# 3x3 taps on TensorE as 64x32 and 32x32 tiles over pairs of rows, one ring of seven PSUM banks, and selections moved in front of the 3x3 evictions

## The chip, the cores and the metric

The kernel runs on one core of a Trainium2 chip. The metric is the device time of one execution in microseconds (us). The kernel before was run three times: 7173.82, 7131.42 and 7154.4 us, median 7154.4. One further execution was profiled, and all traces and rows come from it.

## What is computed

The input x has 8 images of 32 channels and 128x128 pixels. All arithmetic is float32.

```
y  = group_norm(x)                    # 16 groups of 2 channels
xb = for each pixel, the K=8 shifted copies of y (5x5 window) whose 3x3 patches
     differ least: channels 32*8 = 256
h  = relu(dw3x3(conv1x1(xb, w1), w2)) # 256 -> 256 channels, then 3x3 per channel
h  = relu(dw3x3(conv1x1(h, w3), w4))
wi = sigmoid(dw3x3(conv1x1(h, w5), w6))
x1 = x + conv1x1(grouped1x1(wi * grouped1x1(xb, dct_w), inv_dct_w), agg_w)
out = x1 + conv5x5(group_norm(x1), kernel)   # the same 5x5 kernel for all channels
```

## The kernel before, in words

**Steps and turns.** An image is cut into 16 stripes of 8 rows (R), and a 17th, short step (n = NS = 16) finishes the rows that the 3x3 convolutions still owe. That makes 136 steps, 128 of them full. The main loop (L918 on) runs over the steps s, and in each step over four turns, i in (3, 2, 1, 0). Turns 3, 2 and 1 are the three conv layers, each on another stripe: layer 1 on step s, layer 2 on step s-1, layer 3 on step s-2. Turn 0 ends stripe s-2: the dct product (`final_dct`, L747), then, in the next turn, the aggregation and the addition (`final_add`, L763).

**A conv layer.** The 1x1 convolution has 256 output channels. Channels 128 to 255 ("v") are made by `pointwise_v` (matmuls L637 into banks `pv`, ACT's copies L645 into the buffer `tv`), and their 3x3 taps run on DVE: the first tap is an ACT activation (L685), the other eight are DVE instructions (L688), and an activation on ACT (L692) ends them. Channels 0 to 127 ("t") are made by `pointwise_t` (matmuls L660 into banks `p`, ACT's copies L667 into the buffer `t`), and their 3x3 taps run on TensorE (`depthwise_t`, L700 on): the partitions of `t` hold four rows of 32 channels each, and the weights `dwd` are diagonal blocks over 96 or 128 partitions, so that a matmul with 32 output columns sums three vertical taps at once. Each bank `pw` holds four of the stripe's eight rows (`u` chooses which), and takes 3 horizontal taps x 4 groups of 32 channels = 12 matmuls; the second one needs a block of zero weights. ACT reads both banks with the layer's function (L721). Rows that a stripe shares with its neighbours are copied within `t` by DMAs on SP's queue: L670 and L672 after the 1x1 convolution, and `rows_before_t` (L616) after the eviction. A float32 matmul is two passes in the trace.

**The gather.** Each turn also works on a unit of four rows and four of the eight copies. `gather_load` (L544) has POOL load the lists `ib` (and, now and then, the pixels `xt`). `gather_select` (L578) makes 0/1 selections of them on ACT: a Square (L584) and a Relu (L585) for each of two halves, four activations of 1024 elements. `gather_pixels` (L588) multiplies pixels by selections on TensorE (44 matmuls L599 into a bank `pg`), and ACT copies the bank to `xb` (L606).

**Other work.** For the next image, a queue of tasks runs the patch costs (DVE L410, ACT L418, TensorE L425 into its own bank) and the top-8 search; for the image that has just ended the 5x5 convolution (TensorE L836, `layer1`). `tick` gives out credit for the tasks, and `run` takes tasks from the four queues D, P, A and Q at fixed places of a turn.

**PSUM.** Eight banks: a ring of five (`ps_x`) shared by `pv`, `p`, `pg`, `pc`, `pa` and the 5x5 and setup products, one (`ps_d`) for the patch costs, and two (`ps_dw`) that only `depthwise_t` uses. A tile of the ring takes the slot whose last tile is oldest, and its first matmul waits until that tile has been read.

**Order.** PE, DVE and ACT execute in the order of the program text (`manual_schedule`, the set ORDERED); on POOL and SP the scheduler places the instructions. `depthwise_v` and `depthwise_t` are generators, and each `next` runs one piece: `next(dv)` is the activation L692 of the layer started one turn before, `next(dt)` first its 3x3 matmuls and, at the second call, its evictions L721. In a turn with i > 0 the order before is: `pointwise_v` (and the first tap L685 of the new layer), `final_add` if it is due, queue P, queue Q, `gather_select` of unit u+1, `gather_load` of unit u+3, `tick`, DVE's taps of the new layer, `pointwise_t`, `rows_before_v` of an older layer, `gather_pixels` of unit u, the 3x3 matmuls L709 of the layer started one turn before, queue A, its L692, its L721. In turn 0 `final_dct` stands behind queue P, and the 3x3 matmuls stand ahead of `gather_pixels`.

Of the kernel before, what the change touches and what calls it, by code (L numbers as in the profile page):

```python
# [16 lines left out]
P = 128  # L17
# [3 lines left out]
R = 8  # L21
# [22 lines left out]
def bm3d_conv_preact(  # L44
# [27 lines left out]
        tc.tile_pool(name="ps_x", bufs=5, space=bass.MemoryType.PSUM)  # L72
# [37 lines left out]
    dwd = const.tile([P, 3, 2, 4, 3, C], F32, name="dwd")  # L110

    tb = [const.tile([P, 4, 4, W], F32, name=f"t{i}") for i in range(3)]
# [32 lines left out]
    with tc.tile_pool(name="setup", bufs=1) as sp, tc.tile_pool(  # L147
        name="setup_ps", bufs=2, space=bass.MemoryType.PSUM
    ) as spp:
        dwt = sp.tile([P, 3, 4, 9], F32, name="dwt")  # L150
        for n, w in enumerate((w2, w4, w6)):
            for g in range(4):
                nc.sync.dma_start(
                    dwt[C * g : C * (g + 1), n],
                    w[:P].rearrange("(q c) o a b -> c q (o a b)", c=C),
                )
            nc.gpsimd.memset(dwd[0:C, n, 1], 0.0)
            for u in range(2):
                for dy in range(3):
                    s = slice(C * (u + dy), C * (u + dy + 1))  # L160
                    nc.gpsimd.tensor_tensor(
                        dwd[s, n, u],
                        cst[s, C_M32 : C_M32 + C]
                        .unsqueeze(1)
                        .unsqueeze(1)
                        .to_broadcast([C, 4, 3, C]),
                        dwt[s, n, :, 3 * dy : 3 * dy + 3].unsqueeze(3).to_broadcast([C, 4, 3, C]),
                        ALU.mult,
                    )
# [13 lines left out]
        for name, dst in (("w1", lw1), ("w3", lw3), ("w5", lw5)):  # L183
            for g in range(2):
                ps = spp.tile([P, CK], F32, name=f"ps_{name}_{g}", tag="ps")
                for m in range(2):
                    src = wide[name][:, m, g * P : (g + 1) * P]
                    nc.tensor.transpose(ps[:, m * P : (m + 1) * P], src, ident)
                nc.scalar.copy(dst[:, g], ps)
# [3 lines left out]
    ps_dw = ctx.enter_context(  # L193
        tc.tile_pool(name="ps_dw", bufs=1, space=bass.MemoryType.PSUM)
    )
# [416 lines left out]
    def rows_before_t(i, b, n):  # L612

        t = tb[i - 1]
        if n < NS:
            nc.sync.dma_start(t[0:64, :, 0], t[64:P, :, 3])  # L616
# [30 lines left out]
    def pointwise_t(i, b, n, lhsT, src):  # L647
        t = tb[i - 1]
        nb = 2 if n < NS else 1
        if n == NS and i == 1:  # L650
            nc.gpsimd.memset(t[:, :, 2], 0.0)
        else:
            for q in range(2):
                ps = ps_x.tile([P, 2, 2, W], F32, name=f"p{i}_{b}_{n}_{q}", tag="x")
                for e in range(2):
                    s = slice(C * (2 * q + e), C * (2 * q + e + 1))
                    for g in range(2):
                        rows = src(g)
                        for r in range(4):
                            nc.tensor.matmul(  # L660
                                ps[C * r : C * (r + 1), e, :nb],
                                lhsT[:, g, s],
                                rows[:, r : r + 4 * nb - 3 : 4],
                                start=g == 0,
                                stop=g == 1,
                            )
                nc.scalar.copy(t[:, 2 * q : 2 * q + 2, 2 : 2 + nb], ps[:, :, :nb])  # L667
            for r in range(i - 1) if n == 0 else range(i - 1, 4) if n == NS else ():
                nc.gpsimd.memset(t[C * r : C * (r + 1), :, 2], 0.0)
        nc.sync.dma_start(t[64:P, :, 0:nb], t[0:64, :, 2 : 2 + nb])  # L670
        if nb == 2:
            nc.sync.dma_start(t[0:64, :, 1], t[64:P, :, 2])  # L672

    def depthwise_v(i, b, n):
        v = tv[i - 1]
        nr = R if n < NS else 4
# [19 lines left out]
    def depthwise_t(i, b, n):  # L696
        t = tb[i - 1].rearrange("p q (h k) w -> p q h k w", k=2)
        nb = 2 if n < NS else 1

        pt = [  # L700
            ps_dw.tile([P, 2, 2, W], F32, name=f"pw{i}_{b}_{n}_{u}", tag=f"dw{u}")
            for u in range(2)
        ]
        for u in range(2):
            hi = 96 if u == 0 else P
            for dx in (0, -1, 1):
                xa, xz = max(0, -dx), min(W, W - dx)
                for j in range(4):
                    nc.tensor.matmul(  # L709
                        pt[u][C * j : C * (j + 1), :, :nb, xa:xz],  # L710
                        dwd[0:hi, i - 1, u, j, dx + 1],
                        t[0:hi, j, :, :nb, xa + dx : xz + dx],
                        start=dx == 0,
                        stop=True,
                        skip_group_check=True,
                    )
        yield 1
        acc = accp.tile([P, R, W], F32, name=f"acc{i}_{b}_{n}_0", tag=f"acc{i}0")
        rows = acc.rearrange("p (k e) w -> p e k w", e=4)
        for u in range(2):  # L720
            nc.scalar.activation(rows[:, u:4:2, :nb], pt[u][:, :, :nb], funcs[i - 1])  # L721
# [179 lines left out]
    with tc.manual_schedule(engines=ORDERED):  # L901
# [15 lines left out]
        for s in range(len(steps) + 2):  # L917
# [10 lines left out]
            for i in (3, 2, 1, 0):  # L928
# [23 lines left out]
                if s < len(steps):  # L952
                    unit(gather_select, u + 1)
# [8 lines left out]
                if s < len(steps):  # L962
                    unit(gather_pixels, u)
                    u += 1
# [3 lines left out]
                next(dv, None)  # L968
                next(dt, None)
# [70 lines left out]
```

## Time and profile before

The profiled execution took 7131.18 us; its span, from the first to the last instruction, is 7129.4 us, and the mean granted TensorE clock was 0.978.

| what | us |
|---|---|
| profiled execution | 7131.18 |
| its span | 7129.4 |
| runs | 7131.42, 7154.4, 7173.82 |
| DVE, eight taps of v (L688), 3264 instructions | 4084.0 |
| PE, selections times pixels (L599), 45056 passes | 593.6 |
| PE, 1x1 for t from `acc` (L660), 17408 passes | 994.1 |
| ACT, copies of `xb` (L606), 512 | 303.6 |
| ACT, copies of `tv` (L645), 784 | 444.8 |
| ACT, copies of `t` (L667), 800 | 423.0 |

How to read the profile: busy time is the union of an engine's instructions; PE and PEld (weight loads) are kept apart and run beside each other. PEclk is the TensorE clock that was granted, in tenths, over 40 equal slices of the span. A row of a group gives line, engine, operation, output and inputs with their shape, count, then busy time, mean ns of one, and the idle time just ahead of these instructions with what ended most of it. Matmuls run beside one another on tiles of the array, so that a group's mean duration times its count is far above its busy time. In a stretch of the timeline a row is start (us), length, engine, line and group, and the number of instructions.

### The profile page before, as it was taken

Reading aid. Unit: us, or ns where it says so; the run is one execution under the profiler, and the core shown is the slowest. Engines: PE = TensorE matmul, PEld = TensorE weight load, DVE = VectorE, ACT = ScalarE, POOL = GpSimd, SP = SyncE. Lnnn points to the kernel's source line nnn. Section 1 sums busy time; section 2 is a strip of 40 time slices with the busy share of each in tenths; the row PEclk is TensorE's granted clock in tenths of the full one; section 3 lists DMA queues with packets and bytes.
Section 4 is the critical chain, followed back from the end, with each engine's and each line's share of the span. In section 5 each row is a group of like instructions: output and inputs, shape, how many; then the busy total and the mean of one; then the engine's idle time right before and its main releaser. Section 6 shows DMA issues by size and latency. Waiting matters only on the chain. (4 is left out here: it accounts for less than half of the span.)

```text
span 7129.4 us, 229485 instructions
## 1 busy us (share of the span) xinstructions
PE 6700.9 (94%) x100226; PEld 3166.8 (44%) x100226; DVE 5840.1 (82%) x8606; ACT 5061.7 (71%) x6706; POOL 2738.3 (38%) x4599
## 2 busy tenths in 40 slices
PE   4699999999999999999999999999999999999997
PEld 1344444444444444444444444444444444444443
DVE  6689978888888898878888898888978889767675
ACT  4687768677686777867677776877768677666762
POOL 6244336333353343533335343543335333232222
PEclk8899999999999999999999999999999999999999
DMA  3566756666565575666656666566656666555652
GB/s 81 130 145 151 155 129 153 142 148 149 134 156 143 138 166 125 160 145 145 154 127 160 141 152 140 142 161 150 152 130 150 151 145 147 125 146 139 149 134 63
DMA packets 765484, 1007.70 MB, mean 141 GB/s; under 512 B 215008, under 2 KB 578592, under 8 KB 764480
## 3 DMA queue, kind: packets, MB, share of 16 engines
q0 software_dynamic: 378400, 733.67, 42.5%
q1 hardware_dynamic: 381056, 256.86, 17.0%
q8 instruction: 788, 12.91, 0.8%
q10 hardware_dynamic: 5024, 2.49, 0.2%
q14 instruction: 216, 1.77, 0.1%
HBM read 542.24 MB, written 217.01 MB: 106 GB/s over the span
## 5 line engine op out<-in xcount | busy, mean ns | idle before, releaser
L688 DVE SCALAR_TENSOR_TENSOR acc<-tv,dwv,acc 128x1024 f32<-128x1024 f32 (+1 forms) x3264 | 4084.0, 1253 | 223.1 <-ACT acc L685 109.5
L709 PE MATMUL pw<-t,dwd 128*32 128x508 f32 (+6 forms) x19584 | 2179.5, 592 | 156.8 <-DMA t<-t 109.4
L709 PEld LDWEIGHTS pw<-t,dwd 128*32 128x32 f32 (+1 forms) x19584 | 702.3, 111 | 1393.8 <-issue 1205.9
L570 POOL DMA_DIRECT2D ib<-idxd x1024 | 575.2, 563 | 1881.5 <-ACT sel L585 1764.8
L584 ACT ACTIVATE ib<-ib,nplace 128x1024 bf16<-128x1024 bf16 x1024 | 1165.4, 1138 | 25.6 <-DMA ib<-idxd 25.6
L585 ACT ACTIVATE sel<-ib 128x1024 f32<-128x1024 bf16 x1024 | 1084.4, 1059 | 32.6
L660 PE MATMUL p<-acc,lw 128*32 128x256 f32 x17408 | 994.1, 375 | 10.3 <-issue 10.0
L637 PE MATMUL pv<-acc,lw 128*128 128x512 f32 (+1 forms) x2112 | 971.9, 602 | 10.5 <-DVE acc L760 6.3
L606 ACT COPY xb<-pg 128x512 f32<-128x512 f32 x512 | 303.6, 593 | 713.5 <-PE pg L599 713.1
L645 ACT COPY tv<-pv 128x512 f32<-128x512 f32 (+2 forms) x784 | 444.8, 584 | 482.0 <-PE pv L637 463.6
L660 PEld LDWEIGHTS p<-acc,lw 128*32 128x32 f32 x17408 | 562.8, 110 | 429.6 <-issue 81.0
L721 ACT ACTIVATE acc<-pw 128x512 f32<-128x512 f32 (+1 forms) x816 | 452.8, 584 | 341.2 <-PE pw L709 340.8
L599 PEld LDWEIGHTS pg<-sel,xt 128*32 128x32 f32 x45056 | 591.2, 111 | 225.7 <-issue 126.1
L599 PE MATMUL pg<-sel,xt 128*32 128x48 f32 x45056 | 593.6, 206 | 82.9 <-issue 53.1
L780 DVE TENSOR_TENSOR xr<-xr,pa 128x256 f32<-128x256 f32 (+2 forms) x136 | 55.1, 405 | 717.9 <-PE pa L773 698.8
L637 PEld LDWEIGHTS pv<-acc,lw 128*128 128x128 f32 x2112 | 381.0, 191 | 407.7 <-issue 376.7
L410 DVE TENSOR_TENSOR df<-xn 128x786 f32<-128x786 f32 (+2 forms) x576 | 529.0, 969 | 17.2 <-PE pd L425 14.6
L667 ACT COPY t<-p 128x512 f32<-128x512 f32 x800 | 423.0, 570 | 119.8 <-PE p L660 116.5
L418 ACT ACTIVATE df<-df 128x786 f32<-128x786 f32 (+2 forms) x576 | 461.1, 862 | 50.4 <-DVE df L410 49.3
L685 ACT ACTIVATE acc<-tv,dwv 128x1024 f32<-128x1024 f32 (+1 forms) x408 | 459.8, 1127 | 45.8 <-PE pa L773 32.1
L637 PE MATMUL pv<-xb,lw 128*128 128x512 f32 x1024 | 475.7, 607 | 0.0
L757 PE MATMUL pc<-xf,ldct 128*128 128x512 f32 (+2 forms) x1056 | 470.9, 588 | 0.0
(128 smaller groups left out, 6397.3 us busy)
## 6 DMA issues: line engine op xcount, KB each, us to landing
ib<-idxd POOLq DMA_DIRECT2D x1024, 256.0 KB
xbd<-xb POOLq DMA_DIRECT2D x128, 1024.0 KB
xf<-xbd POOLq DMA_DIRECT2D x480, 256.0 KB
t<-t SPq DMA_DIRECT2D x792, 128.0 KB, 4.8
t<-t SPq DMA_DIRECT2D x384, 256.0 KB, 4.9
tv<-tv SPq DMA_DIRECT2D x384, 130.0 KB, 4.1
xt<-xtd POOLq DMA_DIRECT2D x240, 176.0 KB
xl<-xs POOLq DMA_DIRECT2D x256, 64.0 KB
```

The source lines that it names most:

```text
L410: nc.vector.tensor_sub(df[:, :, ca:cz], xn[:, r0 : r0 + SR, ca:cz], xn[:, r0 + dy : r0 + dy + SR, ca + dx : cz + dx],)
L418: nc.scalar.activation(df[:, :, ca:cz], df[:, :, ca:cz], AF.Square)
L570: nc.gpsimd.dma_start(ib.rearrange("p k y x -> p (k y x)"), idxd[b][s4 // 8, s4 % 8, 4 * k0 : 4 * k0 + 8] .rearrange("k x -> (k x)") .part ...
L584: nc.scalar.activation(ib, ib, AF.Square, bias=nplace)
L585: nc.scalar.activation(sel, ib, AF.Relu, scale=-1.0, bias=1.0)
L599: nc.tensor.matmul(pg[C * j : C * (j + 1), :, xa:xz], xt[:, t], sels[j // 2][:, j % 2, :, xa:xz], start=True, stop=True,)
L637: nc.tensor.matmul(ps[:, :hr], lhsT[:, g, P:CK], src(g)[:, h : h + hr], start=g == 0, stop=g == 1,)
L660: nc.tensor.matmul(ps[C * r : C * (r + 1), e, :nb], lhsT[:, g, s], rows[:, r : r + 4 * nb - 3 : 4], start=g == 0, stop=g == 1,)
L685: nc.scalar.activation(acc, rows, AF.Copy, scale=tap)
L688: nc.vector.scalar_tensor_tensor(acc, rows, tap, acc, op0=ALU.mult, op1=ALU.add)
L709: nc.tensor.matmul(pt[u][C * j : C * (j + 1), :, :nb, xa:xz], dwd[0:hi, i - 1, u, j, dx + 1], t[0:hi, j, :, :nb, xa + dx : xz + dx], start ...
L757: nc.tensor.matmul(ps[:, : z - a], ldct[:, m], xf[:, m, a:z], start=True, stop=True)
```

## The change

- `depthwise_t` takes four banks of the common ring in place of two of its own. Part (h, e) holds the rows 4h + e and 4h + e + 2 of the stripe, 256 elements a partition. A partition half (64 partitions, h) now holds one pair of rows in each of three slots of `t` (before: four rows over 128 partitions in four slots). The first half of the matmuls (`single` = 0) takes two vertical taps at once, with 64 partitions and 32 columns; the second half takes the third vertical tap, with 32 partitions and 32 columns. That is 2 x 3 x 2 x 4 x 2 = 96 matmuls of 256 columns in place of 24 of 512.
- `pointwise_t` sorts its rows accordingly, and issues one DMA (`t[64:P, :, 0]` from `t[0:64, :, 2]`) in place of two. Buffers `dwd` and `t` change shape; the zero blocks of `dwd` go.
- The evictions (before L721) become four of 256 elements in place of two of 512.
- `ps_x` has seven banks in place of five; `ps_dw` is gone, and setup uses the ring.
- In the last step of an image `depthwise_v` computes i rows in place of 4, and `pointwise_t` and `depthwise_t` only the rows that count.
- `gather_select` of unit u+1 stands behind queue A and L692 and ahead of the evictions, in place of ahead of `gather_load`. `u` advances there.

The diff, without the setup of the weights:

```diff
@@ -69,7 +69,7 @@
         tc.tile_pool(name="dram", bufs=2, space=bass.MemoryType.DRAM)
     )
     ps_x = ctx.enter_context(
-        tc.tile_pool(name="ps_x", bufs=5, space=bass.MemoryType.PSUM)
+        tc.tile_pool(name="ps_x", bufs=7, space=bass.MemoryType.PSUM)
     )
     ps_d = ctx.enter_context(
         tc.tile_pool(name="ps_d", bufs=1, space=bass.MemoryType.PSUM)
@@ -107,11 +107,11 @@
-    dwd = const.tile([P, 3, 2, 4, 3, C], F32, name="dwd")
-    tb = [const.tile([P, 4, 4, W], F32, name=f"t{i}") for i in range(3)]
+    dwd = const.tile([P, 3, 3, 4, 3, C], F32, name="dwd")
+    tb = [const.tile([P, 4, 3, W], F32, name=f"t{i}") for i in range(3)]
     tv = [const.tile([P, R + 2, W + 2], F32, name=f"tv{i}") for i in range(3)]
...
@@ -190,9 +186,6 @@
     xbp = ctx.enter_context(tc.tile_pool(name="xb", bufs=2))
     accp = ctx.enter_context(tc.tile_pool(name="acc", bufs=1))
-    ps_dw = ctx.enter_context(
-        tc.tile_pool(name="ps_dw", bufs=1, space=bass.MemoryType.PSUM)
-    )
     dsum = keep.tile([P, R + 2, W + 2], F32, name="dsum")
@@ -613,7 +606,7 @@
         t = tb[i - 1]
         if n < NS:
-            nc.sync.dma_start(t[0:64, :, 0], t[64:P, :, 3])
+            nc.sync.dma_start(t[0:64, :, 0], t[64:P, :, 2])
         else:
             nc.gpsimd.memset(t[0:64, :, 0], 0.0)
@@ -646,34 +639,36 @@
     def pointwise_t(i, b, n, lhsT, src):
         t = tb[i - 1]
-        nb = 2 if n < NS else 1
-        if n == NS and i == 1:
-            nc.gpsimd.memset(t[:, :, 2], 0.0)
-        else:
-            for q in range(2):
-                ps = ps_x.tile([P, 2, 2, W], F32, name=f"p{i}_{b}_{n}_{q}", tag="x")
-                for e in range(2):
-                    s = slice(C * (2 * q + e), C * (2 * q + e + 1))
-                    for g in range(2):
-                        rows = src(g)
-                        for r in range(4):
-                            nc.tensor.matmul(
-                                ps[C * r : C * (r + 1), e, :nb],
-                                lhsT[:, g, s],
-                                rows[:, r : r + 4 * nb - 3 : 4],
-                                start=g == 0,
-                                stop=g == 1,
-                            )
-                nc.scalar.copy(t[:, 2 * q : 2 * q + 2, 2 : 2 + nb], ps[:, :, :nb])
-            for r in range(i - 1) if n == 0 else range(i - 1, 4) if n == NS else ():
-                nc.gpsimd.memset(t[C * r : C * (r + 1), :, 2], 0.0)
-        nc.sync.dma_start(t[64:P, :, 0:nb], t[0:64, :, 2 : 2 + nb])
-        if nb == 2:
-            nc.sync.dma_start(t[0:64, :, 1], t[64:P, :, 2])
+        nb, nq = (2, 4) if n < NS else (1, 2)
+        if n == NS:
+            nc.gpsimd.memset(t[0:64, :, 1:3], 0.0)
+        for q in range(2 if n < NS or i > 1 else 0):
+            ps = ps_x.tile([P, 2, 2, W], F32, name=f"p{i}_{b}_{n}_{q}", tag="x")
+            for e in range(2):
+                s = slice(C * (2 * q + e), C * (2 * q + e + 1))
+                for g in range(2):
+                    rows = src(g)
+                    for r in range(4 if n < NS else i - 1):
+                        y = 4 * (r // 2) + r % 2
+                        nc.tensor.matmul(
+                            ps[C * r : C * (r + 1), e, :nb],
+                            lhsT[:, g, s],
+                            rows[:, y : y + 2 * nb - 1 : 2],
+                            start=g == 0,
+                            stop=g == 1,
+                        )
+            m = P if n < NS else C * (i - 1)
+            nc.scalar.copy(t[:m, 2 * q : 2 * q + 2, 1 : 1 + nb], ps[:m, :, :nb])
+        if n == 0:
+            for r in range(i - 1):
+                nc.gpsimd.memset(t[C * r : C * (r + 1), :, 1], 0.0)
+        if n < NS:
+            nc.sync.dma_start(t[64:P, :, 0], t[0:64, :, 2])
     def depthwise_v(i, b, n):
         v = tv[i - 1]
-        nr = R if n < NS else 4
+        nr = R if n < NS else i
         out_ = accp.tile([P, R, W], F32, name=f"acc{i}_{b}_{n}_1", tag=f"acc{i}1")
         acc = out_[:, :nr]
         for k, (dy, dx) in enumerate(
@@ -694,31 +689,42 @@
         rows_before_v(i, b, n)
     def depthwise_t(i, b, n):
-        t = tb[i - 1].rearrange("p q (h k) w -> p q h k w", k=2)
-        nb = 2 if n < NS else 1
-        pt = [
-            ps_dw.tile([P, 2, 2, W], F32, name=f"pw{i}_{b}_{n}_{u}", tag=f"dw{u}")
-            for u in range(2)
-        ]
-        for u in range(2):
-            hi = 96 if u == 0 else P
+        t = tb[i - 1]
+        parts = []
+        for h in range(2 if n < NS else 1):
+            for e in range(2):
+                k = 2 if n < NS else (i + 1 - e) // 2
+                if k:
+                    ps = ps_x.tile([P, 2, W], F32, name=f"pw{i}_{b}_{n}_{h}{e}", tag="x")
+                    parts.append((h, e, k, ps))
+        for single in range(2):
             for dx in (0, -1, 1):
                 xa, xz = max(0, -dx), min(W, W - dx)
-                for j in range(4):
-                    nc.tensor.matmul(
-                        pt[u][C * j : C * (j + 1), :, :nb, xa:xz],
-                        dwd[0:hi, i - 1, u, j, dx + 1],
-                        t[0:hi, j, :, :nb, xa + dx : xz + dx],
-                        start=dx == 0,
-                        stop=True,
-                        skip_group_check=True,
-                    )
+                for e in range(2):
+                    for j in range(4):
+                        for h, e_, k, ps in parts:
+                            if e_ != e:
+                                continue
+                            if single:
+                                lo, m, u, p = 64 * h + C * e, C, 2, 1 - e
+                            else:
+                                lo, m, u, p = 64 * h, 64, e, e
+                            nc.tensor.matmul(
+                                ps[C * j : C * (j + 1), :k, xa:xz],
+                                dwd[lo : lo + m, i - 1, u, j, dx + 1],
+                                t[lo : lo + m, j, p : p + k, xa + dx : xz + dx],
+                                start=dx == 0 and not single,
+                                stop=True,
+                                skip_group_check=True,
+                            )
         yield 1
         acc = accp.tile([P, R, W], F32, name=f"acc{i}_{b}_{n}_0", tag=f"acc{i}0")
-        rows = acc.rearrange("p (k e) w -> p e k w", e=4)
-        for u in range(2):
-            nc.scalar.activation(rows[:, u:4:2, :nb], pt[u][:, :, :nb], funcs[i - 1])
+        for h, e, k, ps in parts:
+            y = 4 * h + e
+            nc.scalar.activation(acc[:, y : y + 2 * k - 1 : 2], ps[:, :k], funcs[i - 1])
         rows_before_t(i, b, n)
         accs[i, b, n][0] = acc
@@ -950,7 +956,6 @@
                 run("Q")
                 if s < len(steps):
-                    unit(gather_select, u + 1)
                     unit(gather_load, u + 3)
                     tick(b, i)
                 next(new_v, None)
@@ -961,11 +966,13 @@
                     next(dt, None)
                 if s < len(steps):
                     unit(gather_pixels, u)
-                    u += 1
                 if i:
                     next(dt, None)
                 run("A")
                 next(dv, None)
+                if s < len(steps):
+                    unit(gather_select, u + 1)
+                    u += 1
                 next(dt, None)
                 kept, dv, dt = dv, new_v, new_t
                 if live and not i:
```

More of the change, by code (lines that the diff above doesn't have):

```diff
@@ L144, in bm3d_conv_preact @@
     nc.vector.tensor_scalar(inner, inner, -1.0, 1.0, op0=ALU.mult, op1=ALU.add)
-    with tc.tile_pool(name="setup", bufs=1) as sp, tc.tile_pool(
-        name="setup_ps", bufs=2, space=bass.MemoryType.PSUM
-    ) as spp:
+    with tc.tile_pool(name="setup", bufs=1) as sp:
         dwt = sp.tile([P, 3, 4, 9], F32, name="dwt")
         for n, w in enumerate((w2, w4, w6)):
[L152 to L155, printed above, removed]
-                )
-            nc.gpsimd.memset(dwd[0:C, n, 1], 0.0)
-            for u in range(2):
[L159 to L168, printed above, removed]
-                    )
+            taps = w[:P].rearrange("(q c) o a b -> c q (o a b)", c=C)
+            for h in range(0, P, 64):
+                nc.sync.dma_start(dwt[h : h + C, n], taps)
+                nc.sync.dma_start(dwt[h + C : h + 64, n, :, 0:6], taps[:, :, 3:9])
+                nc.sync.dma_start(dwt[h + C : h + 64, n, :, 6:9], taps[:, :, 0:3])
+            for u in range(3):
+                nc.gpsimd.tensor_tensor(
+                    dwd[:, n, u],
+                    cst[:, C_M32 : C_M32 + C]
+                    .unsqueeze(1)
+                    .unsqueeze(1)
+                    .to_broadcast([P, 4, 3, C]),
+                    dwt[:, n, :, 3 * u : 3 * u + 3].unsqueeze(3).to_broadcast([P, 4, 3, C]),
+                    ALU.mult,
+                )
         wide = {}
@@ L184, in bm3d_conv_preact @@
             for g in range(2):
-                ps = spp.tile([P, CK], F32, name=f"ps_{name}_{g}", tag="ps")
+                ps = ps_x.tile([P, CK], F32, name=f"ps_{name}_{g}", tag="x")
                 for m in range(2):
@@ L706, in depthwise_t @@
+        for single in range(2):
             for dx in (0, -1, 1):
                 xa, xz = max(0, -dx), min(W, W - dx)
-                for j in range(4):
-                    nc.tensor.matmul(
-                        pt[u][C * j : C * (j + 1), :, :nb, xa:xz],
-                        dwd[0:hi, i - 1, u, j, dx + 1],
-                        t[0:hi, j, :, :nb, xa + dx : xz + dx],
-                        start=dx == 0,
-                        stop=True,
-                        skip_group_check=True,
-                    )
+                for e in range(2):
[15 more added lines that the diff above has]
+                            )
@@ L717, in depthwise_t @@
         yield 1
         acc = accp.tile([P, R, W], F32, name=f"acc{i}_{b}_{n}_0", tag=f"acc{i}0")
-        rows = acc.rearrange("p (k e) w -> p e k w", e=4)
-        for u in range(2):
-            nc.scalar.activation(rows[:, u:4:2, :nb], pt[u][:, :, :nb], funcs[i - 1])
+        for h, e, k, ps in parts:
+            y = 4 * h + e
+            nc.scalar.activation(acc[:, y : y + 2 * k - 1 : 2], ps[:, :k], funcs[i - 1])
         rows_before_t(i, b, n)
```

## Prediction

> **What bounds the kernel now.** I read the page's busy line first, then the costliest groups, then the waits, then one stretch of the timeline for PE and one for ACT. The page says that TensorE is the bound over the whole run:
>
> ```profile
> PE 6700.9 (94%) x100226; PEld 3166.8 (44%) x100226; DVE 5840.1 (82%) x8606; ACT 5061.7 (71%) x6706; POOL 2738.3 (38%) x4599
> ...
> PEclk8899999999999999999999999999999999999999
> ```
>
> PE is idle for only 428 us of 7129.4, at a clock that is full from the third slice on. DVE is busy 82%, so a PE that gets faster by more than a tenth would no longer be the bound. The groups that the change touches:
>
> ```profile
> L688 DVE SCALAR_TENSOR_TENSOR acc<-tv,dwv,acc 128x1024 f32<-128x1024 f32 (+1 forms) x3264 | 4084.0, 1253 | 223.1 <-ACT acc L685 109.5
> L709 PE MATMUL pw<-t,dwd 128*32 128x508 f32 (+6 forms) x19584 | 2179.5, 592 | 156.8 <-DMA t<-t 109.4
> ...
> L584 ACT ACTIVATE ib<-ib,nplace 128x1024 bf16<-128x1024 bf16 x1024 | 1165.4, 1138 | 25.6 <-DMA ib<-idxd 25.6
> L585 ACT ACTIVATE sel<-ib 128x1024 f32<-128x1024 bf16 x1024 | 1084.4, 1059 | 32.6
> ...
> L721 ACT ACTIVATE acc<-pw 128x512 f32<-128x512 f32 (+1 forms) x816 | 452.8, 584 | 341.2 <-PE pw L709 340.8
> ```
>
> The 3x3 taps on PE (L709) are a third of PE's time. The selections (L584, L585) are ACT's largest work, and today their place costs nothing, because ACT idles elsewhere for PE: 713.1 us at L606, 463.6 at L645, 340.8 at L721 in the view of waits. PE's rows in one stretch (start, length, group):
>
> ```profile
> 3057.06 1.09 PE L599 MATMUL pg<-sel,xt 128*32 128x48 f32 x88
> 3057.98 5.33 PE L709 MATMUL pw<-t,dwd 96*32 96x512 f32 x48
> 3063.24 3.70 PE L637 MATMUL pv<-xb,lw 128*128 128x512 f32 x8
> 3066.78 4.42 PE L836 MATMUL p<-xm,band 128*128 128x512 f32 x10
> 3071.12 0.86 PE L425 MATMUL pd<-df,neg 128*32 128x393 f32 x8
> 3071.81 3.63 PE L660 MATMUL p<-xb,lw 128*32 128x256 f32 x64
> ```
>
> Start to start, a 3x3 group takes 5.26 us, pv 3.54, p 3.45, pg 0.92 to 1.04, with no gap. ACT's rows beside them:
>
> ```profile
> 3060.51 0.60 ACT L606 COPY xb<-pg 128x512 f32<-128x512 f32 x1
> 3060.99 1.63 ACT L418 ACTIVATE df<-df 128x786 f32<-128x786 f32 x2
> 3062.49 1.06 ACT L692 ACTIVATE acc<-acc 128x1024 f32<-128x1024 f32 x1
> 3063.44 1.09 ACT L721 ACTIVATE acc<-pw 128x512 f32<-128x512 f32 x2
> 3065.26 0.59 ACT L645 COPY tv<-pv 128x512 f32<-128x512 f32 x1 [0.73 <-PE pv L637]
> 3066.98 0.58 ACT L645 COPY tv<-pv 128x512 f32<-128x512 f32 x1 [1.13 <-PE pv L637]
> 3067.60 1.15 ACT L685 ACTIVATE acc<-tv,dwv 128x1024 f32<-128x1024 f32 x1
> ```
>
> The evictions (L721) are done 1.3 us after the group on PE is, and pv's copies wait for PE.
>
> **The change, part by part.** A step is four turns of the inner loop; 128 of the 136 steps are full. All sums are against the profiled execution, 7131.2 us, which is near the lowest of the three runs (7131.4 to 7173.8, median 7154.4).
>
> *Taps as smaller tiles.* 48 passes of 512 columns in 5.13 to 5.33 us are 12 rounds of four tiles beside each other, 0.427 us a round (pv: 8 passes on the whole array in 3.54). The new group has 96 passes of 256 columns on 8 tiles and 96 on 16: 12 + 6 rounds of half the length, 0.213 each, 3.84 us. I add 0.14 at the end as today (5.26 less 5.12), and 0.1 for each of two more changes of tile shape (pv to p with a change takes 3.63, without one 3.54). New group 4.18; saved 1.08 x 384 full groups = **-415 us**. No row shows tiles that differ in their rows side by side. Bounds: nothing overlaps beyond the four column tiles, 48 rounds of 0.213 = 10.2 us, +1900 us; or the passes of one column strip go in program order, each matmul beginning with its predecessor's second pass: 25 x 0.213 + 0.34 = 5.67 us, +160 us. I take full overlap, since the nearest row, pd, shows it between column tiles: 8 passes of 393 columns (0.33 us each) in 0.86 us is two rounds. Since a matmul's two passes stand next to each other in the program, strict order would need five.
>
> [...]
>
> *Fewer transfers of t* (L670 and L672 become one): SP issues 384 fewer. PE waits 109.4 us for t<-t now; bounds 0 and -121 (with 11.8 for tv<-tv), I take **-60**.
>
> *Evictions:* four of 256 elements (0.375 us, the row of that shape) in place of two of 0.597: +0.31 x 384 = 118 us of ACT, hidden while ACT has idle time; uncovered it is the whole 118. The last step of an image gets shorter on DVE and PE: 0 to -60, I take **-20**. Setup happens once, and its price is under 10 us; nothing.
>
> *The selections and the ring.* Four selections take 4.28 us (3072.44 to 3076.72 in ACT's rows). They now stand behind the relu (L692) and ahead of the evictions, so evictions, pv's copies, L685 (which starts DVE's taps) and the t copies queue behind them. The 3x3 banks are no longer their own: four of seven ring slots. In the new program's order, `pc` matmuls wait 200 times (of 544) for an eviction of pw2, `p3` 202 times (of 272) for one of pw1, and pw1's fourth bank waits in 119 steps for DVE's multiply out of `pc`. Before, no p, pa, pc or pg had to wait so. The walk, from a pg's end: copy 0.5 (+0.2 to begin), squares 1.5 in about half the turns, relu 0.95, selections 4.28, first eviction 0.37: 6.3 us, or 7.8 with squares.
>
> - pc after pw2: PE reaches the second pc at 4.18 + 0.88 = 5.05. Wait 1.2 or 2.8, take 2.0, x 128 = +256.
> - p3 after pw1, pg, pv3, pa: PE is there at 3.54 + 1.0 = 4.55. Wait 1.7 or 3.2 unless an L836 group (4.4 us) lies between, which half the steps have: 2.5 x 64 = +160.
> - p1 after pw3 and pv1: PE at 7.7, banks at 6.3 or 7.8 and later whenever ACT is late: 0.5 x 128 = +64.
> - pw1 after pc: over the 128 full steps, today's first multiply (L760) starts 3.7 us (median; quarters 2.3 and 5.3) after the first pc, since DVE still runs its taps. So the second multiply ends at about 5.1. PE arrives 2 x 1.08 earlier and loses 2.0 of it at pc: 5.3, where the bank is wanted at 3.53 + 0.43 = 4.0. Wait 1.3 at the median, and the late quarter pays 2.9 and more: mean 2.2 x 119 = +262.
>
> Together **+742**; bounds 0 (ACT runs ahead) and about +1000 (every wait at its upper value). POOL's loads of ib now wait for later selections, and xf, xbd and x1d stand behind them; they are used a step or two turns later (13 us a turn), so nothing, with up to +60 if that cover goes.
>
> Sum: -415 - 60 - 20 + 742 = +247: 7131 + 247 = 7378; on the runs' median (23 above the profiled time) 7400.
>
> **Rivals.**
> - *Ring waits decide (forecast)*: 7400, between 7250 and 7700. For it: 94% PE means that each wait counts; against it: ACT has 2068 us of idle time.
> - *Row tiles don't overlap within a column strip*, so the change does not do what it says: +160, with the waits shrinking as each pw ends 1.5 us later (pc 0.5 x 128, p3 160, DVE 60: 284): +160 - 60 - 20 + 284, on the median about 7520. For it: no row with it. With no overlap at all, near 9000.
> - *ACT runs ahead (faster)*: PE's saving stays. The place is the second pc and pw1's fourth bank; if ACT uses its idle time to be done by then, waits fall to a third, 250: -415 - 80 + 250, on the median about 6900. It decides against me from waits under 495/128 = 3.9 us a step; I have 5.8. For it: 340.8 us at L721 that the selections can fill; against it: L606 waits for pg in the same turn, so the selections cannot start sooner.
> - *Gain and waits cancel*: 7154.
>
> **How the numbers follow.** Forecast 0.55, no row overlap 0.22, ACT ahead 0.17, cancel 0.06. Predicted is the likeliest, 7400. The range runs from 7080 (the cancel case, and the faster case's edge) to 7800 (the first rival with its waits at their upper value); what is left out is most of the 0.17 and the 0.03 near 9000. Differences under 0.5% are about what a measurement of this kernel cannot tell from none: faster 0.17, same 0.06, slower 0.77.
>
> **What would show it.** Tiles right: the 3x3 row takes 4.0 to 4.4 us start to start and its busy time falls to some 1700 us; at 5.6 the first rival holds. Ring right: the waits list PE pc, p and pw behind ACT's evictions and DVE's L760 multiply, 4 us or more a step, PE's share falls under 88%, and L721's successor no longer waits for PE. Wrong would be: PE still over 92%, or the time lost at transfers.

## The result, and the profile after

The changed kernel took 7885.77 us (median of 4 runs, 7871.45 to 7948.51) against 7155.5 us for the kernel before (now 4 runs): a ratio of 1.1049, 95% interval 1.102 to 1.1078. It is slower by a tenth: the sign is the forecast one, and the time lies past the upper end of the range (7800). The profiled execution has a span of 7873.0 us at a mean granted clock of 0.953 (before 7129.4 and 0.978).

The page of the changed kernel, its busy line, the instruction queue, and the groups of the 3x3 taps on PE, the taps on DVE and the evictions (columns as before):

```profile
PE 6905.0 (88%) x155650; PEld 3853.1 (49%) x155650; DVE 5796.1 (74%) x8606; ACT 5103.6 (65%) x7466; POOL 2719.6 (35%) x4563
...
PEclk7899999999999999999999999999999999999999
...
q8 instruction: 1222, 20.02, 1.1%
...
L683 DVE SCALAR_TENSOR_TENSOR acc<-tv,dwv,acc 128x1024 f32<-128x1024 f32 (+3 forms) x3264 | 4032.8, 1237 | 357.3 <-ACT acc L680 252.7
L715 PE MATMUL pw<-t,dwd 64*32 64x254 f32 (+3 forms) x75648 | 2189.8, 386 | 302.5 <-issue 162.3
...
L727 ACT ACTIVATE acc<-pw 128x256 f32<-128x256 f32 (+1 forms) x1576 | 469.7, 380 | 84.2 <-PE pw L715 83.1
```

By the sum PE was to become 415 us less busy, and it is 204 us busier; the 3x3 group, L715, is at 2189.8 us where L709 was at 2179.5. PE's idle time rose from 428 to 968 us, and the largest releaser in front of L715 is "issue", which means that PE waited for nothing that the profile can name. The line that I had passed over stands under the DMA queues (queue, kind: packets, MB, share of 16 engines). On the page of the kernel before it reads:

```profile
q8 instruction: 788, 12.91, 0.8%
```

So instructions come to PE by DMA. 20.02 MB in 1222 packets is 16 KB each, and 1222 x 256 = 312,832 against 313,007 PE instructions in the trace (weight loads, matmul passes and others): a packet is a piece of 256 PE instructions, 64 bytes for each. The change multiplies the instructions of a 3x3 group by four (48 weight loads and 48 passes; then 192 and 192), so PE needs a new piece 1222 times and not 788 times.

The view of the waits of PE in the changed kernel (waiting engine and line, releaser: us in total, times, longest):

```profile
PE pg L592 <- issue: 237.2, 84, 9.8
PE pw L715 <- issue: 162.3, 195, 5.5
PE pw L715 <- DVE acc L766: 125.5, 53, 6.1
PE p L654 <- ACT acc L727: 71.1, 35, 4.3
...
PE pc L763 <- ACT acc L727: 33.8, 21, 4.5
```

The same view of the kernel before has little for issue, and none of the three ring waits (pw behind DVE, p and pc behind the evictions):

```profile
PE pg L599 <- issue: 53.1, 36, 4.7
...
PE pw L709 <- issue: 27.2, 16, 5.4
```

Where an issue wait falls is seen in PE's timeline, at one stretch of 9.7 us (start, length, group, count, and in brackets the idle time ahead):

```profile
753.65 0.46 PE L592 MATMUL pg<-sel,xt 128*32 128x48 f32 x24
761.92 1.46 PE L592 MATMUL pg<-sel,xt 128*32 128x48 f32 x64 [7.80 <-issue]
```

PE stops after 24 of the 88 passes of one product, for 7.80 us. Its first eight passes have already used every buffer that the 88 read, and all write the same bank, so that no wait for another engine can stand between the 24th and the 25th. In the trace's DMA records the next instruction packet starts at 758.84 and takes 1.69 us; PE resumes 1.39 us after it has landed. A second stretch shows what follows a stop:

```profile
3068.76 3.44 PE L715 MATMUL pw<-t,dwd 64*32 64x254 f32 x128 [1.12 <-issue]
3074.42 1.09 PE L715 MATMUL pw<-t,dwd 32*32 32x254 f32 x13 [2.22 <-issue]
3075.44 6.35 PE L630 MATMUL pv<-xb,lw 128*128 128x512 f32 x8
```

The packet of the second stop starts at 3072.10, takes 0.95, and PE resumes 1.37 us after it; the eight passes of pv then take 6.35 us, where 3.70 was shown before. The clock records of the trace know two values, 1 and 0.5. Here the record says half clock from 3073.98 for 6.83 us; from 300 us on, all but one of the 134 such stretches are a slice of 3.41 us or several.

I took all gaps of PE over 0.15 us from 300 us on and matched them with the packets of the instruction queue. A gap that ends 1.1 to 1.75 us after a piece has landed is called a supply stall below (the expectations put on record first use an earlier count, 412 us and 78 for the 431 and 91 of the table):

| profiled execution | before | after |
|---|---|---|
| supply stalls, us (number) | 91.0 (56) | 431.2 (307) |
| other gaps of PE, us | 172.7 | 381.4 |
| time at half clock, us | 186.4 | 612.9 |
| PE busy at half clock (whole span), us | 210.3 | 556.8 |

Over the whole span all gaps together grew by 540 us: supply stalls +340 and others +209 by the table, which leaves the start out. Work at half clock takes twice its time (at the median, passes of pv start 0.854 us apart at half clock and 0.429 at full), so that +347 us of it cost 173. 540 + 173 = 713 of the 744 us by which the spans differ; the other 31 are more work of PE. If busy time at half clock is counted half, the 3x3 matmuls alone stand at 2126 us against 2121, though an undisturbed group is 0.47 us shorter (4.79 against 5.26), 180 us in all. An undisturbed new group in the timeline, and what starts behind it:

```profile
1084.23 4.86 PE L715 MATMUL pw<-t,dwd 64*32 64x256 f32 x192
1089.02 1.55 PE L763 MATMUL pc<-xf,ldct 128*128 128x512 f32 x3
```

Such groups are the smaller part. Of 162 new groups at full clock in which no gap over 0.15 us falls, 65 take under 4.85 us, and the median is 5.03. With the gaps taken out, the 340 groups at full clock take 176 us more in all than at 4.79 each, so the saving is lost inside the groups. It goes with the pieces: of the 162, 15 of the 17 in which no new piece comes into use are under 4.85 us, and 50 of the 145 others. So part of the price of late pieces doesn't show as gaps.

**Why the pieces are late.** Counting PE's instructions in the trace, the k-th packet starts at the earliest when PE has begun 256k + 145 of them, and at the latest at 256k + 449, where PE stands. So a piece is asked for 304 instructions before PE runs dry, at best. At the median 217 are left in the kernel before, 173 in the changed one. From a packet's start to the instructions' use it takes 2.4 to 2.8 us in half of the supply stalls of the changed kernel, and 2.1 at the least (1.1 us for the packet at the median of all 1222, and 1.3 to 1.5 after it in half of the stalls). An undisturbed new 3x3 group has 384 instructions in 4.79 us, 12.5 ns each: 173 of them last 2.2 us. The old one has 96 in 5.26 us, and 217 instructions reached far beyond it. The product pg, which stands next to the group, is denser still in both kernels: 88 weight loads and 88 passes in 0.92 to 1.04 us. With the longer group beside it, this is where the largest issue wait falls.

### The profile page after: what moved, and what is told of

It is laid out like the page before. It is cut to its first block, busy times and chain, and to the rows that moved or that the text cites. A ratio compares the mean times of both kernels' runs of the same rounds, so it can differ in the third digit from the quotient of the medians.

```text
span 7873.0 us, 340650 instructions
## 1 busy us (share of the span) xinstructions
PE 6905.0 (88%) x155650; PEld 3853.1 (49%) x155650; DVE 5796.1 (74%) x8606; ACT 5103.6 (65%) x7466; POOL 2719.6 (35%) x4563
## 3 DMA queue, kind: packets, MB, share of 16 engines
q8 instruction: 1222, 20.02, 1.1%
## 5 line engine op out<-in xcount | busy, mean ns | idle before, releaser
L683 DVE SCALAR_TENSOR_TENSOR acc<-tv,dwv,acc 128x1024 f32<-128x1024 f32 (+3 forms) x3264 | 4032.8, 1237 | 357.3 <-ACT acc L680 252.7
L715 PE MATMUL pw<-t,dwd 64*32 64x254 f32 (+3 forms) x75648 | 2189.8, 386 | 302.5 <-issue 162.3
L715 PEld LDWEIGHTS pw<-t,dwd 64*32 64x32 f32 (+1 forms) x75648 | 1338.5, 106 | 1076.7 <-issue 597.8
L630 PE MATMUL pv<-acc,lw 128*128 128x512 f32 (+1 forms) x2112 | 1049.1, 642 | 3.9 <-issue 3.9
L592 PE MATMUL pg<-sel,xt 128*32 128x48 f32 x45056 | 617.3, 209 | 283.9 <-issue 237.2
L662 ACT COPY t<-p 128x512 f32<-128x512 f32 x800 | 444.5, 577 | 456.3 <-PE p L654 444.1
L630 PEld LDWEIGHTS pv<-acc,lw 128*128 128x128 f32 x2112 | 411.8, 207 | 444.0 <-issue 428.4
L727 ACT ACTIVATE acc<-pw 128x256 f32<-128x256 f32 (+1 forms) x1576 | 469.7, 380 | 84.2 <-PE pw L715 83.1
L763 PE MATMUL pc<-xf,ldct 128*128 128x512 f32 (+2 forms) x1056 | 492.1, 605 | 35.3 <-ACT acc L727 33.8
L654 PE MATMUL p<-xb,lw 128*32 128x256 f32 x8192 | 483.1, 389 | 28.9 <-DVE xy L853 20.0
L687 ACT ACTIVATE acc<-acc 128x1024 f32<-128x1024 f32 (+3 forms) x408 | 415.4, 1018 | 143.5 <-DVE acc L683 143.3
```

The lines of the kernel that those rows point to most:

```text
L592: nc.tensor.matmul(pg[C * j : C * (j + 1), :, xa:xz], xt[:, t], sels[j // 2][:, j % 2, :, xa:xz], start=True, stop=True,)
L630: nc.tensor.matmul(ps[:, :hr], lhsT[:, g, P:CK], src(g)[:, h : h + hr], start=g == 0, stop=g == 1,)
L654: nc.tensor.matmul(ps[C * r : C * (r + 1), e, :nb], lhsT[:, g, s], rows[:, y : y + 2 * nb - 1 : 2], start=g == 0, stop=g == 1,)
L662: nc.scalar.copy(t[:m, 2 * q : 2 * q + 2, 1 : 1 + nb], ps[:m, :, :nb])
L683: nc.vector.scalar_tensor_tensor(acc, rows, tap, acc, op0=ALU.mult, op1=ALU.add)
L715: nc.tensor.matmul(ps[C * j : C * (j + 1), :k, xa:xz], dwd[lo : lo + m, i - 1, u, j, dx + 1], t[lo : lo + m, j, p : p + k, xa + dx : xz + dx],
```

## The experiments

All times are medians; each ratio is to runs of the kernel before on the same chip, with its 95% interval. Theories, as the expectations name them: supply (PE runs out of instructions), ring (four of seven common banks), place (the selections in front of the evictions).

**Selections back in front.** In the changed kernel:

```diff
                 run("Q")
                 if s < len(steps):
+                    unit(gather_select, u + 1)
                     unit(gather_load, u + 3)
...
                 next(dv, None)
-                if s < len(steps):
-                    unit(gather_select, u + 1)
-                    u += 1
                 next(dt, None)
```

> The changed kernel with the selections back in their old place, ahead of the loads; taps, ring and evictions stay as changed. Supply theory (PE runs out of instructions: in the trace of the changed kernel PE resumes 1.1 to 1.75 us after a 16 KB piece on the instruction queue has landed in 412 us of its gaps, 78 before): those gaps and the half-clock time (613 us, 186 before) stay within a quarter, and at most the other waits go, so 7600 to 7850. Place theory (late selections make the ring late, and PE's gaps start there): the time falls by more than half of the 742, to 7150 to 7450. Ring theory (four slots for the 3x3 parts are the cost, wherever the selections stand): 7700 to 7900.

7846.74 us, 1.0999 (1.0966 to 1.1033): 39 us less than the changed kernel, with overlapping intervals. Supply stalls 550, other gaps 239, half clock 651.

```profile
PE pg L592 <- issue: 318.2, 94, 9.1
PE pw L715 <- issue: 207.4, 168, 8.4
```

The waits at p go, those at pc fall from 33.8 to 6.2 us, and supply stalls take their place: moving the selections back does not give the 730 us back. (The stalls were expected to stay within a quarter and grew by more, from 431 to 550; the theory had left out that one stop hides another.)

**Late selections alone.** The same move in the kernel before.

> The kernel before with only the selections moved behind the activation L692, ahead of the evictions. Place theory: +200 us or more, 7350 to 7600, with PE waiting for ACT at p, pv or pg. Supply theory: PE's instructions are the same, so 7130 to 7250. Ring theory: the 3x3 banks are their own, so evictions may come late at no cost: 7130 to 7250.

7178.05 us, 1.0059 (1.0038 to 1.008): 43 us, six hundredths of the loss. PE waits for the selections at pg, and at pw for evictions:

```profile
PE pg L599 <- ACT sel L585: 68.5, 44, 10.4
PE pw L709 <- ACT acc L721: 39.4, 25, 3.0
...
PE pw L709 <- DMA t<-t: 25.4, 13, 5.1
```

and it waits 84 us less for t<-t than the 109.4 before, since it comes later. One wait stands in for another.

**Instructions alone.** In the kernel before, each 3x3 matmul is cut into four of one row of 128 columns:

```diff
-                for j in range(4):
-                    nc.tensor.matmul(
-                        pt[u][C * j : C * (j + 1), :, :nb, xa:xz],
+                for hh in range(2):
+                    for kk in range(nb):
+                        for j in range(4):
+                            nc.tensor.matmul(
+                                pt[u][C * j : C * (j + 1), hh, kk, xa:xz],
...
```

> The kernel before with each 3x3 matmul cut into four of 128 columns: 96 matmuls a group instead of 24, so as many PE instructions as in the changed kernel, while tiles, banks, evictions and selections stay as before, and the columns that the array takes are the same. Supply theory: the stalls that end after an instruction piece lands rise from 78 to some 300 to 450 us, half-clock time with them, 7450 to 7750. Ring and place theories: nothing that they name is changed, 7100 to 7220, unless a matmul of 128 columns has a price of its own, which would show as a longer 3x3 group without stalls (5.26 us start to start now).

7790.26 us, 1.09 (1.0863 to 1.0938). Banks, evictions, selections and the 128x32 and 96x32 tiles are those of before, and nearly nine tenths of the loss is there (655 of 730 us). Supply stalls 547 us, half clock 501. The waits of PE:

```profile
PE pg L599 <- issue: 307.8, 107, 8.8
PE pw L711 <- issue: 210.8, 203, 7.6
PE pw L711 <- DMA t<-t: 60.0, 47, 10.6
```

A price of the small matmul itself is in it too, but little: an undisturbed group takes 5.33 us and not 5.26, 0.07 x 384 = 27 us of the 655.

**The ring alone.** In the kernel before, one ring of seven, the two 3x3 banks in it:

```diff
-        tc.tile_pool(name="ps_x", bufs=5, space=bass.MemoryType.PSUM)
+        tc.tile_pool(name="ps_x", bufs=7, space=bass.MemoryType.PSUM)
...
-            ps_dw.tile([P, 2, 2, W], F32, name=f"pw{i}_{b}_{n}_{u}", tag=f"dw{u}")
+            ps_x.tile([P, 2, 2, W], F32, name=f"pw{i}_{b}_{n}_{u}", tag="x")
```

> The kernel before with one ring of seven banks in which the two 3x3 banks take two slots; tiles, instructions and the selections' place stay. Ring theory: PE waits for evictions and for DVE's multiply at pc, p and pw, +150 to +350 us, 7300 to 7500. Supply theory: same instructions, 7100 to 7220. Place theory: selections are early, so the ring costs little, 7100 to 7220.

7142.47 us, 1.0006 (0.9991 to 1.0021): nothing. The ring together with late selections was not run in the kernel before.

**Without the largest burst of data.** In the changed kernel, xf is filled once, and its four transfers of 256 KB a step go:

```diff
-        for g in range(2):
-            for m in range(2):
-                nc.gpsimd.dma_start(
-                    xf[64 * g : 64 * (g + 1), m, j0:j1], src[g, m, :, :, ya:yz]
-                )
-        return xr, xf, j0, j1
+        if not xfs:
+            xf = xfs[0] = xbp.tile([P, 2, R, W], F32, name="xf", tag="xf", bufs=1)
+            nc.gpsimd.memset(xf, 0.5)
+        return xr, xfs[0], j0, j1
```

> The changed kernel without the transfers xf<-xbd (four of 256 KB a step): the dct product reads a buffer filled once with a constant, all else stays. If PE's instruction pieces come late because their packets wait behind this data, the stalls that end after a piece has landed fall from 412 us to about 200 (214 of them have xf transfers started in the 9 us before), the half-clock time with them, and the time to 7500 to 7650. If they come late because each is asked for too late whatever else moves, the stalls stay over 350 and the time at 7750 to 7880.

7556.17 us, 1.0606 (1.0574 to 1.0638), 330 us less than the changed kernel (316 by the two ratios). Supply stalls fall to 157, half clock to 366. With as many instructions, PE now stops for others:

```profile
PE pw L715 <- DVE acc L764: 140.0, 60, 6.1
PE p L654 <- ACT acc L727: 99.7, 58, 4.3
PE pw L715 <- issue: 96.8, 139, 2.4
...
PE pg L592 <- issue: 44.4, 51, 2.3
```

The longest issue waits are 2.3 and 2.4 us, and were 9.8 and 5.5. The supply stalls are of two kinds. In the changed kernel 45 of them, 215 us, belong to packets that started only after PE had stopped, and 262, 217 us, to packets that were under way by then. Without xf there are 3 of the first kind, 9 us, and 202 of the second, 148 us. So this data is what holds the late packets back, and most of the short stalls need no such burst: with 384 instructions in 4.79 us PE can run dry while its next piece is under way.

**A shorter group, as many instructions.** The third vertical tap over 63 of 128 columns a row:

```diff
+                            xw = xa + 63 if single else xz
                             nc.tensor.matmul(
-                                ps[C * j : C * (j + 1), :k, xa:xz],
+                                ps[C * j : C * (j + 1), :k, xa:xw],
...
```

> The changed kernel with the 32x32 tiles (the third vertical tap) over only about half of their columns, 63 of 128 a row: that work is left out, the number of instructions stays. If the second half of a 3x3 group (2.05 us in the undisturbed groups of the changed kernel) is set by the array's columns, it falls to about 1.1 and the time by up to 380 us, 7500 to 7700. If it is set by the pace of the instructions (16.7 ns a pass in the trace), it stays at 1.7 or more, and as the group is no shorter or empties the pieces faster, the time is 7750 to 7900.

7851.97 us, 1.1029 (1.0993 to 1.1064), within the interval of the changed kernel. The undisturbed group did get shorter, from 4.79 to 4.14 us, its second half from 2.05 to 1.40, between the two expectations (1.1 and 1.7). That is 0.65 x 384 = 250 us of PE's work, and the time doesn't move: supply stalls 557, half clock 797. Faster groups meet the end of the piece sooner.

**Half the dose.** In the kernel before, each 3x3 matmul cut into two (192 instructions a group, 941 pieces).

```diff
-                for j in range(4):
+                for hh in range(2):
+                    for j in range(4):
...
-                        pt[u][C * j : C * (j + 1), :, :nb, xa:xz],
+                            pt[u][C * j : C * (j + 1), hh, :nb, xa:xz],
```

> The kernel before with each 3x3 matmul cut into two of 256 columns: 192 weight loads and passes a group, between the 96 of before (78 us of stalls after a piece) and the 384 of the cut into four (536 us, +655 us in time). Supply theory: one piece ahead still covers most of it, so less than a third of the cut into four's: stalls of 120 to 220 us, 7190 to 7310. If each matmul has a price of its own, the time rises by 24/72 of 655 = 218 us or more, 7340 to 7400.

7218.33 us, 1.0114 (1.0075 to 1.0153). 96 instructions a group more cost 92 us, 288 more cost 655: more than in proportion, as is expected of a cover that is used up. Supply stalls 141, half clock 258.

**Half the dose, four slots.** The same with the four parts of 256 elements in slots of one ring of seven, and four evictions.

```diff
-            ps_dw.tile([P, 2, 2, W], F32, name=f"pw{i}_{b}_{n}_{u}", tag=f"dw{u}")
+            [
+                ps_x.tile([P, 2, W], F32, name=f"pw{i}_{b}_{n}_{u}_{hh}", tag="x")
+                for hh in range(2)
+            ]
...
-            nc.scalar.activation(rows[:, u:4:2, :nb], pt[u][:, :, :nb], funcs[i - 1])
+            for hh in range(2):
+                nc.scalar.activation(rows[:, u + 2 * hh, :nb], pt[u][hh][:, :nb], funcs[i - 1])
```

> The same cut into two, and the four parts of 256 elements as in the changed kernel: one ring of seven, four slots of it and four evictions a group, selections early, tiles as before. Ring theory: 100 to 300 us over the cut into two alone, with PE waiting at p, pc and pw. Supply theory: within 50 us of it, since the one ring with two slots cost nothing.

7252.96 us, 1.0178 (1.0142 to 1.0214): 35 us over the run without the ring, with overlapping intervals. The wait that the prediction named appears:

```profile
PE pw L708 <- DVE acc L760: 38.4, 20, 4.0
```

**No xf, early selections.** The run without xf, and the selections back in front.

> The changed kernel without the xf transfers (the dct product reads a constant) and with the selections back in their old place. Without xf, PE still waits 440 us for others than instructions, 100 of them at p for ACT's evictions, 37 at pc, 140 at pw for DVE's multiply. If the selections' place makes these waits and was covered by the instruction stalls until now, p's and pc's go and 7380 to 7480 is left of 7556; if something else makes them, 7520 to 7590.

7291.48 us, 1.0214 (1.0195 to 1.0232): 265 us less than with late selections, and below the 7380 to 7480 expected; in the presence of xf the same move brought 39. So the place has a price after all, and supply stalls cover it: with xf the move took 142 us of other gaps away and added 119 us of supply stalls, without xf it took 225 away and added 48. A likely reason is that ACT gets its selections and evictions done while PE lacks instructions. What is left in PE's waits:

```profile
PE pw L715 <- DVE acc L764: 125.2, 55, 6.1
PE pw L715 <- issue: 116.3, 150, 2.5
PE pg L592 <- issue: 72.5, 67, 2.6
```

**The control.** The kernel before without the xf transfers.

> The kernel before without the xf transfers (the dct product reads a constant): the control for the run without xf. Supply theory: before has 91 us of stalls after an instruction piece, so little is to be had, 7040 to 7120, and the changed kernel's gain of 316 us is an interaction of its instruction count with this data. If the xf data cost PE or DVE in another way, before falls by 200 us or more as well, to 6930 or less.

7025.23 us, 0.9848 (0.9826 to 0.987): 110 us, a little more than expected. Supply stalls 33, half clock 120. So 330 - 110 = some 220 us of the gain without xf (206 by the ratios) come from the change meeting this data. That it is the instruction count that meets it is read from the supply stalls, 431 to 157 us there and 91 to 33 here; the cut into four was not run without xf. Against this control the changed taps and ring, with early selections, still lose 266 us.

**The burst spread, before.** The kernel before, all work kept:

```diff
-        for g in range(2):
-            for m in range(2):
-                nc.gpsimd.dma_start(
-                    xf[64 * g : 64 * (g + 1), m, j0:j1], src[g, m, :, :, ya:yz]
-                )
+        def piece(g, m):
+            nc.gpsimd.dma_start(
+                xf[64 * g : 64 * (g + 1), m, j0:j1], src[g, m, :, :, ya:yz]
+            )
+
+        piece(0, 0)
+        parts[3] = [partial(piece, 1, 0), partial(piece, 0, 1)]
+        parts[2] = [partial(piece, 1, 1)]
...
+                for part in parts.pop(i, ()):
+                    part()
                 if not i and 0 <= s - 1 < len(steps):
                     fins[s - 1] = final_load(*steps[s - 1])
```

> The kernel before with the four xf transfers started in three turns (one, two, one) in place of all four in one turn; all work is kept. If instruction pieces and t<-t wait behind the burst, some 20 to 60 of PE's 91 us of instruction stalls and 109 us for t<-t go, 7070 to 7115; if not the burst but the sum of the data counts, no change, 7120 to 7160.

7207.37 us, 1.01 (1.0083 to 1.0117): slower by 71 us, a miss. Supply stalls stay at 91, PE's wait for t<-t grows from 109.4, and half clock grows from 186 to 286.

```profile
PE pw L709 <- DMA t<-t: 152.7, 61, 11.8
```

Which of the spread transfers delays t<-t was not tried.

**The burst spread, after.** The same edit in the changed kernel, with early selections.

> The changed kernel with early selections and the four xf transfers started in three turns; all work is kept. If the burst is what delays the instruction pieces, the stalls of 550 us (early selections alone, 7847 us) fall to 300 to 400 and the time to 7550 to 7700; if the sum of the data counts, 7780 to 7870. Under no theory does it come under the kernel before.

7730.76 us, 1.0833 (1.0812 to 1.0855), between the expectations: 116 us less than with early selections alone. Supply stalls 465 (550). The stalls of packets that started after PE had stopped fall from 338 to 212 us, where leaving xf out left 8. So the burst is a part; whether the rest is the sum of the data, or that two transfers still start in one turn, is not shown.

No version with all of the work beats the kernel before.

## Why the prediction was wrong, point by point

- **PE is the bound**: right. The loss is PE's idle time and clock: 713 of 744 us.
- **The tiles overlap**: right, and the first rival fell (4.79 us where 5.6 was its sign). Eight 64x32 passes on four columns and two rows of tiles start within 0.05 us of each other, and the next eight 0.214 us later, as the sum had it.
- **New group 4.18 us**: mis-sized. Undisturbed groups take 4.79: 2.74 for the first half (12 rounds of 0.213 and the rest), 2.05 for the second, where 1.28 and some tail were counted. Most 32x32 passes start 16.7 ns apart, so that 16 of them take 0.267 us and not 0.213. So -180 us (0.47 x 384) was to be had, not -415, and even that doesn't show: the row's busy time is 2190 us, where the sign was 1700. The bound with the passes of a column strip in program order, 5.67 us, did not hold here.
- **Transfers -60**: of the right kind, and larger in the trace: the waits for t<-t and tv<-tv went from 121.2 to 2.7 us. But the late selections alone took 84 us of t<-t away in the kernel before; this wait seems to go whenever PE comes later.
- **Evictions +118 hidden, last step -20**: right as far as is seen. The evictions' durations add up to 599 us where they had 477 (1576 x 0.380 and 816 x 0.584); DVE is 44 us less busy. Neither shows at the end.
- **Ring and selections +742**: wrong in size; that the sum of the whole profiled loss is 744 is chance. The places were right (PE at pw behind DVE's multiply, p and pc behind the evictions), the prices not: 125.5, 71.1 and 33.8 us by the trace, or 1.8 us a step (4 or more was the sign), where +262, +224 (160 and 64) and +256 stood. Other gaps than supply stalls grew by 209, or 327 with the transfers' 118 put back. By experiment the ring alone costs 0, late selections 43, four slots 35; without xf, late selections in the changed kernel cost 265. The walk took ACT to start when PE does; while PE waits for instructions, ACT can get ahead, which is the rival "ACT runs ahead", with its cause not foreseen. A count is off too: there are 528 pc matmuls (1056 passes), not 544.
- **The step that failed** is the one that isn't in the sum: the change part by part counted passes and rounds, and never the instructions. The new group was 96 passes on 8 tiles and 96 on 16, priced by what the array takes; that each pass brings a weight load, and that both must be fetched, was given no row, no bound and no rival. The profile had it in three places: x100226 for PEld and PE each, the instruction queue, and issue ahead of pg and pw (53.1 and 27.2 us). In its place the runs showed supply stalls of +340 us and half clock of +173. Not all of the latter is theirs: 249 of the 426 us that half clock grew by follow slices whose idle time was mostly supply stalls.
- **Luck**: the forecast missed by 486 us, about the 513 that it had left out, only because two other errors cancel. PE's own work was to fall by 435 (415 and 20) and rose by 31; the ring was to cost 742 and shows 327 by the trace. So the right sign rests on a cause that the forecast did not have.
- **The rivals**: none was supply. "PE's share under 88%" came true (87.7%), mostly for another reason: a sign that two causes share shows neither.

Open: which DMA engine a late instruction packet stands behind can't be seen, since the records give queues and not engines; that xf's transfers delay it is shown by the runs without them. The 266 us that the changed taps and ring lose without xf are named by the trace (supply stalls +173 over the control, other gaps +53 in all, with 125 at pw behind DVE among them and less for t<-t, the rest half clock and work), and were not taken apart by a run of their own.

## What to carry to other kernels

Count what an engine must fetch, not only what it must compute: divide the instructions of a stretch by its time, and compare what remains of the piece in hand with the time that a new one takes (here 2.4 to 2.8 us in half of the supply stalls, against 173 instructions of 12.5 ns, which last 2.2). The smaller tiles brought more instructions (155650 passes and as many weight loads, 100226 before), and here the cover did not hold; to find out beforehand, cut the old matmuls into as many without changing anything else, as the run with four did. And where waits overlap, undo an edit in a version without the larger wait, or its price stays hidden (39 us against 265).

## What the runs showed of the hardware that I had not expected

- A piece of 256 PE instructions is asked for at most 304 instructions ahead, takes 1.1 us at the median, and is in use 1.3 to 1.5 us after landing in half of the supply stalls. Ahead of pg and pw, PE's longest issue wait was 9.8 us beside the xf transfers and 2.4 without them.
- Of the 175 stretches at half clock from 300 us on in the two kernels, 167 follow when PE was idle for 1.7 us or more of the 3.41 us ahead (median 2.3 before, 2.6 in the changed kernel). The slices stand on a fixed grid of 3.41 us, and the other way round it holds too: from 300 us on, all 144 full-clock slices with 2 us or more of idle time were followed by half clock, as were 3 of some 3760 with less than 1.5 us. Of the 81 in between, 27 were. In 163 of the 167 cases one stop alone was 1.7 us or longer. From 300 us on there are 134 such stretches in the changed kernel, 41 before.
- Most 32x32 passes of 256 columns start 16.7 ns apart (65% at 15 to 18 in the 65 undisturbed groups under 4.85 us), 0.267 us for 16, and six rounds of 16 take 2.05 us in an undisturbed group; 64x32 tiles take 0.214 for a round of 8.
